# Mixture-of-experts tail: pairs with rows of the first 24 chunks first, two thirds of the sums read ahead of the last product

## The chip, the cores and the metric

The kernel runs on one core of one Trainium2 chip. The metric is the device time of one execution in microseconds (us). TensorE is PE in the profile, VectorE is DVE, ScalarE is ACT, GpSimd is POOL and SyncE is SP. SP and ACT also issue plain transfers, POOL the indirect ones.

## What is computed

Three layers follow each other on an image of 2 x 256 channels x 48 x 48 positions: a mix of local attention and convolution, a state-space layer, and a layer of eight experts of which each position uses two. The change is in the last one and in what follows it. In the terms of the reference (its body is given here in short):

```
xn      = layernorm(x)                                  # 4608 positions x 256
logits  = xn @ Wg + bg                                  # 8 experts
e1, e2  = the two best experts, weights by softmax over the two
y[pos]  = x[pos] + sum over e in (e1, e2) of
          weight_e * (gelu(xn[pos] @ W1[e] + b1[e]) @ W2[e] + b2[e])     # 256 -> 1024 -> 256
out     = y as 2 x 256 x 48 x 48
```

All values are float32.

## The kernel before, in words

**Rows and tables.** The 4608 positions are 36 chunks of 128. The state-space layer works through the chunks in order, in groups of 6, 6, 6, 6, 6, 4 and 2. Behind each group `gate` (line 1524) picks the two experts of each position and `put` (line 1676) scatters the normalized row into a table `xs` in HBM, in which each expert has its own part and the rows of an expert stand in the order of the chunks. `taken` counts the rows of each expert. The residual of each chunk goes to `acc` in HBM (`keep`, line 1507), to which the experts add.

**Early tiles.** After four groups, 24 chunks, `early_expert` (line 1691) picks the expert with the most rows so far, and three tiles of 256 rows of it are computed during the last groups (`early_tile`, line 1744: products at lines 1802 and 1818, addition at 1830, scaling at 1837, scatter into `acc` at 1840). `ahead` holds the rows that this takes from that expert, `begin` where the rest of each expert begins.

**Planning.** `plan` (line 1852) turns the counts into two small tables with a chain of DVE instructions on all partitions: for each of 33 pairs (256 rows of one expert) and up to 8 singles (128 rows), the row of the table and the place of the expert's weights. The pairs stand in the order of the experts. The tables lie in the SBUF of the input `x[1]`, and SP reads an entry into a register (`value`, line 1936) ahead of each load.

**The tiles of the experts.** `experts` (line 1950) runs 37 tiles: 33 pairs, with a single behind every eighth pair, so that the last tile is a pair; up to four more singles stand in a branch that is taken only if there are more than four. For tile i, `load` (line 1978) brings the expert's weights (2 MB, a ring of three buffers) and `fetch` (line 1990) its rows; both are issued on SP three tiles ahead. `turn` (line 1997) transposes the rows. `up` (line 2043) makes the first product (line 2051) and the Gelu on ACT (line 2055). `down` makes the second: a single in eight plain products (line 2076) and one addition of the bias (line 2077), a pair in seven products of half the size instead of eight (line 2089, in the manner of Strassen and Winograd), from sums of weights (`weight_sums`, line 2016) and of hidden values (`hidden_sums`, line 2031) that DVE makes, followed by eight additions (lines 2094 to 2102). `finish` (line 2057) scales each 128 x 256 result on ACT (line 2060) and scatters it on POOL with an addition in HBM (line 2061). Two scatters of one tile are not ordered to each other; scatters of different tiles are.

**The results.** `results` (line 2142) runs after the branch. It reads `acc` in twelve blocks of three chunks (line 2152, alternating between SP and ACT) into the SBUF of `x`, transposes them on PE (line 2163), copies each result from PSUM, one half on DVE and one on ACT (line 2166), and writes 128 x 768 values at a time to `out` (line 2169, alternating between SP and ACT).

**What sets the order.** In the layers before, a planner writes the order of PE, DVE, ACT and SP out by cost and due time. In the expert stage the framework orders the instructions of each engine by itself from the order of the program and its dependencies; each engine works through its list in order, and an instruction that waits for a semaphore holds what is behind it. SP reads registers and issues its transfers in program order where the code asks for it. `declare_no_dep` and `add_to_no_dep_group` take the wait between named groups of transfers away.

Of the kernel before, what the change touches and what calls it, by code (L numbers as in the profile page):

```python
# [37 lines left out]
P = 128  # L38
# [26 lines left out]
NJ = 3  # L65
# [13 lines left out]
NUSUAL = E // 2  # L79
NROWS = E * PART + TR  # L80
# [146 lines left out]
class Kernel:  # L227
# [1463 lines left out]
    def early_expert(self, seen):  # L1691
# [9 lines left out]
        def of(name):  # L1701
            return T["e", name]
# [4 lines left out]
                new("count", E), T["before", EARLY + 1][:, 0, :], self.c["base"], ALU.subtract)),  # L1707
            ("DVE", 205, lambda: vec.tensor_reduce(new("most", 1), of("count"), AX.X, ALU.max)),
            ("DVE", 205, lambda: tt(new("hot", E), of("count"), of("most").to_broadcast(wide), ALU.is_equal)),
# [3 lines left out]
            ("POOL", 200, lambda: pool.tensor_tensor(of("count"), of("hot"), self.c["tid"][:, :E], ALU.mult)),  # L1713
# [138 lines left out]
    def plan(self):  # L1852

        nc, begun = self.nc, [5 * TR] * NH
        n, k, tid = P, CAP // TR, self.c["tid"]
        tri = self.c["tri"].rearrange("p (a b) -> p a b", a=E)

        def new(*shape, dtype=F32):
            size = int(np.prod(shape))
            h = next(h for h in range(NH) if begun[h] + size <= N)  # L1860
            t = self.x[1][:, h, begun[h] : begun[h] + size]
            begun[h] += size
            if len(shape) > 1:
                names = "abc"[: len(shape)]
                t = t.rearrange(f"p ({' '.join(names)}) -> p {' '.join(names)}", **dict(zip(names[1:], shape[1:])))
            return t.bitcast(dtype) if dtype != F32 else t

        last_rows = new(E, dtype=I32)
        nc.vector.tensor_scalar(last_rows, self.taken, 1.0, None, ALU.add)
        rows = new(2, E)  # L1870
        nc.vector.tensor_sub(rows[:, 0, :], self.taken, self.begin)
        nc.vector.tensor_scalar(rows[:, 1, :], rows[:, 0, :], float(-P), None, ALU.add)
        full, ab = new(2 * E, k), new(2, E)
        shape = [n, 2 * E, k]
        flat = rows.rearrange("p i e -> p (i e)")
        nc.vector.tensor_tensor(full, bcast(flat, 2, shape), bcast(self.c["thr"], 1, shape), ALU.is_gt)
        nc.vector.tensor_reduce(ab.rearrange("p i e -> p (i e)"), full, AX.X, ALU.add)
        nc.vector.tensor_scalar(ab[:, :, 0:1], ab[:, :, 0:1], 1.0, None, ALU.max)

        def ends(name, count):  # L1880
            each, end = new(E, E), new(E)
            nc.vector.tensor_tensor(each, bcast(count, 1, [n, E, E]), tri, ALU.mult)
            nc.vector.tensor_reduce(end, each, AX.X, ALU.add)
            return end

        def places(name, end, count):

            shape = [n, count, E]
            done, which, begin = new(count, E), new(count), new(count)
            last = new(count, E)  # L1890
            nc.vector.tensor_tensor(done, bcast(tid[:, :count], 2, shape), bcast(end, 1, shape), ALU.is_ge)
            nc.vector.tensor_reduce(which, done, AX.X, ALU.add)
            nc.vector.tensor_tensor(last, done, bcast(end, 1, shape), ALU.mult)
            nc.vector.tensor_reduce(begin, last, AX.X, ALU.max)
            nc.vector.tensor_sub(begin, tid[:, :count], begin)
            return done, which, begin

        pend = ends("p", ab[:, 1, :])
        nc.vector.tensor_scalar(pend, pend, float(NPAIR), None, ALU.min)
        done, pwhich, prow = places("p", pend, NPAIR)  # L1900
        nc.vector.tensor_scalar(prow, prow, float(TR), None, ALU.mult)

        pairs, left = new(E + 1), new(E)
        nc.vector.memset(pairs[:, E:], 0.0)
        nc.vector.tensor_copy(pairs[:, 0:1], pend[:, 0:1])
        nc.vector.tensor_sub(pairs[:, 1:E], pend[:, 1:], pend[:, : E - 1])
        nc.vector.tensor_add(left, ab[:, 0, :], ab[:, 1, :])
        nc.vector.scalar_tensor_tensor(left, pairs[:, :E], -2.0, left, ALU.mult, ALU.add)
        send = ends("s", left)
        many = new(1, dtype=I32)  # L1910
        nc.vector.tensor_copy(many, send[:, E - 1 :])
        done, swhich, srow = places("s", send, NSINGLE)
        step, behind = new(E), new(NSINGLE)
        nc.vector.tensor_sub(step, pairs[:, 1:], pairs[:, :E])
        nc.vector.tensor_tensor(done, done, bcast(step, 1, [n, NSINGLE, E]), ALU.mult)
        nc.vector.tensor_reduce(behind, done, AX.X, ALU.add)
        nc.vector.tensor_scalar(behind, behind, pairs[:, 0:1], 2.0, ALU.add, ALU.mult)
        nc.vector.tensor_add(srow, srow, behind)
        nc.vector.tensor_scalar(srow, srow, float(P), None, ALU.mult)
        where = []  # L1920
        for name, which, row in (("p", pwhich, prow), ("s", swhich, srow)):
            to = new(2, which.shape[-1], dtype=I32)
            nc.vector.scalar_tensor_tensor(row, which, float(PART), row, ALU.mult, ALU.add)
            count = which.shape[-1]
            shape = [n, count, E]
            own, past = new(count, E), new(count)
            nc.vector.tensor_tensor(own, bcast(which, 2, shape), bcast(tid[:, :E], 1, shape), ALU.is_equal)
            nc.vector.tensor_tensor(own, own, bcast(self.ahead, 1, shape), ALU.mult)
            nc.vector.tensor_reduce(past, own, AX.X, ALU.add)
            nc.vector.tensor_add(row, row, past)  # L1930
            nc.vector.tensor_scalar(to[:, 0, :], row, float(E * PART), None, ALU.min)
            nc.vector.tensor_scalar(to[:, 1, :], which, float(E - 1), float(P), ALU.min, ALU.mult)
            where.append(to)
        return last_rows, where, many
# [15 lines left out]
    def experts(self, ctx):  # L1950
# [9 lines left out]
        every = NPAIR // NUSUAL  # L1960
        for i in range(NPAIR):
            tiles.append((2, i))
            if i % every == every - 1:
                tiles.append((1, i // every))
        usual = len(tiles)
        tiles += [(1, i) for i in range(NUSUAL, NSINGLE)]
# [49 lines left out]
        def weight_sums(i):  # L2016


            if i >= len(tiles) or tiles[i][0] == 1:
                return  # L2020
# [36 lines left out]
        def finish(i, y, j):  # L2057
# [7 lines left out]
            self.tc.add_to_no_dep_group(f"tile{i}", put.ins)  # L2065

        def down(i):
# [4 lines left out]
            if tiles[i][0] == 1:  # L2072
                y = hp.tile([P, C], F32, tag="ey", name="ey", bufs=5)
                po = banks[0][:, :C]
                for c in range(NHC):
                    nc.tensor.matmul(po, lhsT=hid[:, c, :P], rhs=w2[:, c, :], start=c == 0, stop=c == NHC - 1)  # L2076
                nc.vector.tensor_add(y, po, b2)
                finish(i, y, 0)
# [40 lines left out]
        def run(first, end):  # L2119
            for i in range(first, end):  # L2120
                up(i)
                if i + 1 < end:
                    turn(i + 1)
                if tiles[i][0] == 2:
                    hidden_sums(i)
                down(i)
                if i + 1 < end:
                    weight_sums(i + 1)
                if i + 3 < end:
                    fetch(i + 3)  # L2130
                    load(i + 3)

        run(0, usual)

        with self.tc.If(self.value(many[0:1, 0:1], list(self.nc.engines), NSINGLE) > NUSUAL):
# [4 lines left out]
            run(usual, len(tiles))  # L2140

    def results(self, ctx):

        nc = self.nc
        op = self.pool("o", 12, ctx)

        blocks = []
        for g in range(B * NBLK):
            b, blk = divmod(g, NBLK)
            t = self.x[b].rearrange("p k n -> p (k n)")[:, blk * NJ * C : (blk + 1) * NJ * C]  # L2150
            t = t.rearrange("p (j c) -> p j c", j=NJ)
            (nc.sync, nc.scalar)[g % 2].dma_start(
                t, self.acc[g * TB : (g + 1) * TB, :].rearrange("(p j) c -> p j c", j=NJ)
            )
            blocks.append(t)
        for g in range(0, B * NBLK, 2):
            b, blk = divmod(g, NBLK)
            for k in range(NH):
                o = op.tile([P, 2, TB], F32, tag="o", name="o")
                for i in range(2):  # L2160
                    ps = self.bank()
                    for j in range(NJ):
                        nc.tensor.transpose(
                            ps[:, j * P : (j + 1) * P], blocks[g + i][:, j, k * P : (k + 1) * P], self.ident
# [6 lines left out]
    def run(self):  # L2171
# [35 lines left out]
        self.ahead = up.tile([P, E], F32, name="ahead")  # L2207
        self.pick = up.tile([P, 4], I32, name="pick")
# [6 lines left out]
        with ExitStack() as end:  # L2215
            self.results(end)
# [87 lines left out]
```

## Time and profile before

| | us |
|---|---|
| median of three runs before | 1310.37 |
| these runs, lowest and highest | 1309.21, 1315.11 |
| the profiled execution, its own time | 1316.04 |
| span of the profiled execution | 1314.3 |
| PE busy | 1232.6 (94%) |
| DVE, ACT, POOL busy | 930.9, 797.9, 557.2 |
| first product of the expert stage begins (line 2051) | 799.77 |
| last product ends (line 2089) | 1277.35 |

The span is the time from the first to the last instruction; the profiled execution's own time is a little longer. The lines of the timeline give the start in us, the length in us, the engine, the line of the kernel, the operation, the destination and source by name, their shapes and how many equal instructions are merged; in brackets stands how long the engine was idle before, and what ended that. SPq and ACTq are the instructions that issue transfers; their length is that of the issuing and not of the transfer. A table of stretches gives, for a stretch, its length, the busy time and number of instructions of PE, PEld (weight loads), DVE, ACT and POOL, the granted clock of PE as a share of full speed, the busy share of the 16 DMA engines and the GB/s they moved.

### The profile page before, as it was taken

The numbers are of one execution on the slowest core, as the hardware profiler recorded it, in microseconds if no ns is written. First come the engines' busy times: TensorE is split into PE (matmuls) and PEld (weight loads), VectorE is DVE, ScalarE is ACT, GpSimd is POOL, SyncE is SP. The second block draws the span as 40 slices with busy tenths as digits, with TensorE's granted clock in tenths as the row PEclk, the third lists the DMA queues.
The fourth block names the chain that finished last, engine by engine and source line by source line (L and its number), as shares of the span: only waits on it lengthen the run. The fifth ranks groups of instructions, "written<-read, shape, count | busy, mean of one in ns | idle before, by whom it ended". The sixth has DMA issues, their size and how long they took to land.

```text
span 1314.3 us, 23601 instructions
## 1 busy us (share of the span) xinstructions
PE 1232.6 (94%) x8072; PEld 981.6 (75%) x8072; DVE 930.9 (71%) x2427; ACT 797.9 (61%) x1957; POOL 557.2 (42%) x769
## 2 busy tenths in 40 slices
PE   4999999996999999999999979999999999999983
PEld 3566767664667766677666758999999999999982
DVE  5899999998587878888878644565565556556642
ACT  2598978897899887987787633233334333332332
POOL 4312230211367798989888872122212121221220
PEclk9999999999899999999999999999999999999997
DMA  8331322210232242426346147567756766776628
GB/s 295 109 103 41 123 75 88 64 49 30 71 93 84 87 140 85 145 80 193 111 139 181 58 140 255 174 212 230 227 177 227 236 200 190 229 236 185 211 39 297
DMA packets 101659, 194.13 MB, mean 148 GB/s; under 512 B 10635, under 2 KB 82652, under 8 KB 96604
## 3 DMA queue, kind: packets, MB, share of 16 engines
q1 hardware_dynamic: 84156, 166.15, 37.7%
q0 software_dynamic: 14400, 19.74, 7.7%
q10 hardware_dynamic: 2980, 6.69, 1.3%
q8 instruction: 66, 1.08, 0.3%
q14 instruction: 57, 0.47, 0.1%
HBM read 154.24 MB, written 43.23 MB: 150 GB/s over the span
## 4 chain that ended last, share of the span: by engine, by line
PE 40%; POOL 10%; DMA 5%; issue 3%; ACT 3%; DVE 3%; SPq 0%; ACTq 0%; DVEq 0%; POOLq 0%
PE bank L2051 17%; PE po L2089 14%; DMA acc<-ey,token 4%; POOL xs L1676 3%; POOL sq L1455 1%; PE bank L914 1%; POOL y L1440 1%; PE bank L1818 1%; PE bank L900 1%; PE zbank L914 1%; POOL y L1422 1%; PE bank L1802 1%; PE bank L1448 1%; PE po L2076 1%; DMA out<-o 1%
## 5 line engine op out<-in xcount | busy, mean ns | idle before, releaser
L2061 POOL DMA_INDIRECT acc<-ey,token x70 | 109.1, 1559 | 370.3 <-ACT ey L2060 330.4
L2051 PE MATMUL bank<-ext,wt 128*128 128x256 f32 (+1 forms) x1152 | 241.3, 368 | 0.0
L2055 ACT ACTIVATE hid<-bank,bt 128x256 f32<-128x256 f32 (+1 forms) x288 | 132.9, 463 | 170.4 <-PE bank L2051 166.4
L2051 PEld LDWEIGHTS bank<-ext,wt 128*128 128x128 f32 x1152 | 207.0, 190 | 25.0
L679 POOL COPY kp<-kp 128x10 f32<-128x10 f32 (+1 forms) x60 | 24.7, 411 | 178.8 <-DVE kp L672 178.8
L590 DVE SCALAR_TENSOR_TENSOR x<-hid,w2r,x 128x1128 f32<-128x1128 f32 (+3 forms) x72 | 100.0, 1394 | 0.4 <-ACT hid L584 0.2
L2089 PE MATMUL po<-ts,ss 128*128 128x128 f32 x792 | 99.2, 275 | 0.0
L914 PE MATMUL bank<-xn,win 128*128 128x387 f32 x240 | 92.4, 508 | 2.1 <-ACT t L996 2.1
L2089 PEld LDWEIGHTS po<-ts,ss 128*128 128x128 f32 x792 | 93.7, 192 | 0.0
L1126 DVE SCALAR_TENSOR_TENSOR xc<-bank,vec,xc 128x384 f32<-128x384 f32 x144 | 86.7, 612 | 9.3 <-ACT xc L1115 8.7
L1342 ACT ACTIVATE mt<-mt,cum 128x128 f32<-128x128 f32 x288 | 88.2, 395 | 0.0
L798 ACT ACTIVATE prob<-prob,top 128x308 f32<-128x308 f32 x144 | 78.6, 554 | 15.7 <-DVE top L787 15.5
L2093 ACT COPY u<-po 128x128 f32<-128x128 f32 x33 | 8.8, 267 | 117.0 <-PE po L2089 117.0
L1676 POOL DMA_INDIRECT xs<-u,rows x72 | 72.6, 1009 | 16.1 <-issue 14.4
L2038 DVE TENSOR_TENSOR ss<-hid 128x512 f32<-128x512 f32 x33 | 22.8, 691 | 72.7 <-ACT hid L2055 72.7
L1448 PE MATMUL bank<-wout,y 128*128 128x264 f32 x288 | 70.8, 390 | 1.2 <-DVE yi L1407 1.2
L914 PE MATMUL zbank<-xn,win 128*128 128x384 f32 x192 | 71.0, 491 | 0.3 <-ACT z L1244 0.3
L804 ACT ACTIVATE prob<-prob,rden 128x308 f32<-128x308 f32 x144 | 68.0, 552 | 3.6 <-DVE rden L853 3.6
L580 DVE SCALAR_TENSOR_TENSOR hid<-xp,vec,hid 128x1175 f32<-128x1175 f32 (+1 forms) x48 | 68.5, 1427 | 0.1
L2089 PE MATMUL po<-wt,hid 128*128 128x128 f32 x512 | 67.6, 275 | 0.0
L787 DVE CUSTOM_DVE_ANT_0 prob<-banks,cst 128x308 f32<-128x308 f32 x144 | 61.7, 473 | 3.9 <-PE banks L777 3.6
L2089 PEld LDWEIGHTS po<-wt,hid 128*128 128x128 f32 x512 | 62.3, 192 | 0.1
(324 smaller groups left out, 2972.6 us busy)
## 6 DMA issues: line engine op xcount, KB each, us to landing
wt<-in_We SPq DMA_DIRECT2D x36, 2048.0 KB
mt<-decays SPq DMA_DIRECT2D x36, 512.0 KB
ex<-xs SPq DMA_DIRECT2D x36, 265.0 KB
rd<-decays SPq DMA_DIRECT2D x68, 128.0 KB
val<-vtab SPq DMA_DIRECT2D x72, 110.0 KB
bt<-in_We SPq DMA_DIRECT2D x36, 136.0 KB
vraster<-vout SPq DMA_DIRECT2D x18, 256.0 KB
acc<-x SPq DMA_DIRECT2D x36, 128.0 KB
```

The costliest lines, as they stand in the source:

```text
L580: nc.vector.scalar_tensor_tensor(dst, src, w[:, k : k + 1], dst, ALU.mult, ALU.add)
L590: nc.vector.scalar_tensor_tensor(dst, src, w[:, k : k + 1], dst, ALU.mult, ALU.add)
L798: nc.scalar.activation(t, t, AF.Exp, bias=T["top", c][:, a : a + 1], scale=-1.0, accum_out=T["den", c][:, a : a + 1])
L914: self.nc.tensor.matmul(ps, lhsT=lhs(k), rhs=rhs(k), start=k == 0, stop=k == NH - 1)
L1126: nc.vector.scalar_tensor_tensor(out(), T["bank", ("cv", at)][:, i : i + TB], wc[:, i : i + 1], out(), ALU.mult, ALU.add)
L1342: nc.scalar.activation(t, t, AF.Relu, bias=at_s, scale=-1.0)
L1448: nc.tensor.matmul(ps[:, : C + E], lhsT=T["y", c][:, m, :], rhs=self.l1["wout"][:, m, :], start=m == 0, stop=m == NZ - 1,)
L1676: ins = nc.gpsimd.indirect_dma_start(self.xs, bass.IndirectOffsetOnAxis(ap=of("rows")[:, i, q : q + 1], axis=0), T["u2", g][:, i, :], None,)
L2051: nc.tensor.matmul(ps[:, :rows], lhsT=w1[:, k, c * P : (c + 1) * P], rhs=xt[:, k, :], start=k == 0, stop=k == NH - 1,)
L2055: nc.scalar.activation(hid[:, c, :], ps[:, :rows], AF.Gelu, bias=bt[:, c : c + 1])
L2061: put = nc.gpsimd.indirect_dma_start(self.acc, bass.IndirectOffsetOnAxis(ap=token[:, j : j + 1], axis=0), y, None, compute_op=ALU.add)
L2089: nc.tensor.matmul(p[name], lhsT=v[a][:, c], rhs=v[w][:, c], start=c == 0, stop=c == NHC // 2 - 1)
```

## The change

- **Order of the pairs.** `plan` gets a second count for each expert: the pairs with a row of the first 24 chunks (`seen`, now kept, less `ahead`, in units of 256 rows, rounded up, and at most the pairs that the expert has). The table of pairs lists these of all experts first, at most 28 of them by the counts, and then the rest of all experts, so that it has up to 16 parts instead of 8. The number of pairs and singles stays.
- **Singles.** A single stands behind every seventh of the first 28 pairs, so the last five tiles are pairs whose rows are all of later chunks.
- **Reads of the first 24 chunks.** The eight blocks of the first 24 chunks are read from `acc` behind the loads of the last tile, all on SP. Their wait for the scatters of the last five tiles is taken away. Blocks 6 to 11 go to another part of `x[1]`. The branch for more singles reads the eight blocks once more at its end.
- **Last tile.** The last pair is computed with plain products in two halves, without the sums of weights and of hidden values.
- **Results.** They no longer have buffers of their own but use the ring of the weights, five of 128 x 768 in one. The last four blocks are read, in program order, behind the code of the first eight.

The core of the diff; the planning is cut to what counts the pairs:

```diff
+BEFORE = sum(GROUPS[: EARLY + 1])
+NFIRST = (BEFORE * 2 * P - NEARLY * TR) // TR + E - 1
...
+        rows = new(3, E)
...
+        vec.tensor_sub(rows[:, 2, :], self.seen, self.ahead)
+        full, ab = piece(3 * E, k), new(3, E)
...
+        first = ab[:, 2, :]
+        vec.tensor_tensor(first, first, ab[:, 1, :], ALU.min)
...
+        pend, second = new(2 * E), new(E)
+        vec.tensor_sub(second, ab[:, 1, :], first)
+        ends(pend[:, :E], first)
+        ends(pend[:, E:], second)
+        vec.tensor_tensor(pend[:, E:], pend[:, E:], pend[:, E - 1 : E].to_broadcast([n, E]), ALU.add)
+        vec.tensor_scalar(pend, pend, float(NPAIR), None, ALU.min)
+        done, pwhich, prow = places(pend, NPAIR)
+        late = new(NPAIR)
+        vec.tensor_scalar(late, pwhich, float(E), None, ALU.is_ge)
+        vec.scalar_tensor_tensor(pwhich, late, float(-E), pwhich, ALU.mult, ALU.add)
...
-        every = NPAIR // NUSUAL
+        every = NFIRST // NUSUAL
         for i in range(NPAIR):
             tiles.append((2, i))
-            if i % every == every - 1:
+            if i < NFIRST and i % every == every - 1:
                 tiles.append((1, i // every))
         usual = len(tiles)
+        last_pairs = usual - (NPAIR - NFIRST)
+        nfirst, load_sums = BEFORE // NJ, self.load_sums
...
-            if i >= len(tiles) or tiles[i][0] == 1:
+            if i >= len(tiles) or tiles[i][0] == 1 or i == usual - 1:
                 return
...
             self.tc.add_to_no_dep_group(f"tile{i}", put.ins)
+            if last_pairs <= i < usual:
+                self.tc.declare_no_dep(put.ins, group="first sums", reason="the last pairs have rows of later chunks")
...
-            if tiles[i][0] == 1:
-                y = hp.tile([P, C], F32, tag="ey", name="ey", bufs=5)
-                po = banks[0][:, :C]
-                for c in range(NHC):
-                    nc.tensor.matmul(po, lhsT=hid[:, c, :P], rhs=w2[:, c, :], start=c == 0, stop=c == NHC - 1)
-                nc.vector.tensor_add(y, po, b2)
-                finish(i, y, 0)
+            if i not in sums:
+                for j, bank in enumerate(banks):
+                    y = hp.tile([P, C], F32, tag="ey", name="ey", bufs=5)
+                    po = bank[:, :C]
+                    for c in range(NHC):
+                        nc.tensor.matmul(
+                            po, lhsT=hid[:, c, j * P : (j + 1) * P], rhs=w2[:, c, :], start=c == 0, stop=c == NHC - 1
+                        )
+                    nc.vector.tensor_add(y, po, b2)
+                    finish(i, y, j)
...
                 if i + 3 < end:
                     fetch(i + 3)
                     load(i + 3)
+                if i + 4 == usual:
+                    for g in range(nfirst):
+                        load_sums(g, "first sums")
...
             turn(usual)
             run(usual, len(tiles))
-
-    def results(self, ctx):
+            for g in range(nfirst):
+                load_sums(g)
+        self.results(ew)
+
+    def sums_block(self, g):
+
+        b, at = divmod(g, NBLK)
+        if b == 0:
+            t = self.flat(0)[:, at * NJ * C : (at + 1) * NJ * C]
+        else:
+            i, h = divmod(at, NH)
+            t = self.x[1][:, h, i * NJ * C : (i + 1) * NJ * C]
+        return t.rearrange("p (j c) -> p j c", j=NJ)
+
+    def load_sums(self, g, group=None):
...
+        get = (nc.sync, nc.scalar)[g % 2 if group is None else 0].dma_start(
+            self.sums_block(g), self.acc[g * TB : (g + 1) * TB, :].rearrange("(p j) c -> p j c", j=NJ)
+        )
+        if group:
+            self.tc.add_to_no_dep_group(group, get.ins)
+
+    def results(self, pool):
...
+        first, size, n = BEFORE // NJ, 2 * TB, 0
         for g in range(0, B * NBLK, 2):
             b, blk = divmod(g, NBLK)
+            if g == first:
+                for i in range(first, B * NBLK):
+                    self.load_sums(i)
             for k in range(NH):
-                o = op.tile([P, 2, TB], F32, tag="o", name="o")
+                if n % (WMAT // size) == 0:
+                    space = pool.tile([P, WMAT], F32, tag="wt", name="o")
+                o = space[:, n % (WMAT // size) * size :][:, :size].rearrange("p (i t) -> p i t", i=2)
+                n += 1
```

## The prediction

> **What bounds the kernel now.** I read the page first, for which engine fills which part of the span, then the timeline and busy time by stretch for the last 50 us, then the timeline around the start of the expert stage, where the enlarged planning runs.
>
> ```profile
> span 1314.3 us, 23601 instructions
> ...
> PE   4999999996999999999999979999999999999983
> ...
> DMA  8331322210232242426346147567756766776628
> ```
>
> Each digit is a fortieth of the span, 32.9 us. PE is full until the last slice but one; the last slice has PE at 3 and DMA at 8. So PE sets the pace until the last product, and something with the DMA engines sets it after that. The timeline shows the joint:
>
> ```profile
> 1276.29 1.06 PE L2089 MATMUL po<-wt,ss 128*128 128x128 f32 x8
> ...
> 1278.70 0.75 DVE L2102 TENSOR_TENSOR ey<-ey,bt 128x256 f32<-128x256 f32 x2
> ...
> 1281.80 1.55 POOL L2061 DMA_INDIRECT acc<-ey,token  x1 [0.31 <-issue]
> ...
> 1285.77 6.05 SPq L2152 DMA_DIRECT2D x<-acc  x6
> 1286.07 7.07 ACTq L2152 DMA_DIRECT2D x<-acc  x6
> ...
> 1294.64 0.34 ACTq L2169 DMA_DIRECT2D out<-o  x1
> ...
> 1306.46 0.34 ACTq L2169 DMA_DIRECT2D out<-o  x1
> ```
>
> The last product ends at 1276.29 + 1.06 = 1277.35 us. Then come the sums of the seven products on DVE, the scaling on ACT and two scatters on POOL, the second ending at 1281.80 + 1.55 = 1283.35. The first read of the sums (line 2152) starts 2.42 us later, once the scatter has landed. From 1285.77 to 1314.3, 28.53 us, twelve reads and twelve writes of 384 KB run. The whole tail behind the last product is 1314.3 - 1277.35 = 36.95 us. By stretch (columns: stretch, length, busy time of PE, PEld, DVE, ACT, POOL, PE clock, DMA share, GB/s):
>
> ```profile
> 1277.50:1285.60 8.10, 0.00 (x0) 0.00 (x0) 1.93 (x8) 0.91 (x2) 3.10 (x2) 0.71 0.29 32
> 1285.60:1288.00 2.40, 0.00 (x0) 0.00 (x0) 0.00 (x0) 0.00 (x0) 0.00 (x0) 0.50 0.48 126
> 1288.00:1311.00 23.00, 12.00 (x72) 9.47 (x72) 7.66 (x12) 7.16 (x12) 0.00 (x0) 0.80 1.02 394
> 1311.00:1314.30 3.30, 0.00 (x0) 0.00 (x0) 0.00 (x0) 0.00 (x0) 0.00 (x0) 0.50 0.09 37
> ...
> 1255.00:1257.00 2.00, 2.00 (x20) 2.00 (x19) 1.13 (x2) 0.00 (x0) 0.00 (x0) 1.00 0.00 0
> ```
>
> For 23 us the DMA share is 1.02: the tail is bound by bytes at 394 GB/s, with 2.40 us of start and 3.30 us of run-out. The last line is inside the last tiles: PE full, DMA 0, since no weights are left to load. The change puts reads there.
>
> **What the Trainium skill says.** "DMA: Bandwidth & Descriptors", section "Issuing engines are not separate DMA queues", says that transfers issued by SP, ACT and POOL end up on the same 16 DMA engines; the trace agrees, the 23 us being full with two issuers. Its section "Anatomy of one DMA — SWDGE (gpsimd) path" puts about 2.0 us of a transfer down to fixed cost, mostly confirmation of the write; the 2.42 us between scatter and read agrees. "Perfetto Trace Analysis", "Sequencer Loop", has a sequencer read its next instruction and wait for its semaphores, which is why I looked at what stands behind each new wait; the first ACT copy of the results idling 13.3 us behind DMA x<-acc fits that.
>
> **The change, part by part.** I call the end of the last product T (1277.35) before and T' after.
>
> *Eight reads moved.* They stand on SP behind the weights of the last pair, which before are issued at 1243.37, when the buffer of three tiles earlier comes free. Three pairs then follow, each with a pitch of 13.60 us (two starts of line 2051: 1202.38 and 1215.98). Nothing else stands behind them on SP before the branch. They bring 8 x 384 KB = 3.15 MB into a stretch with about 41 us. With the last pair's 2.3 MB this is 5.5 MB, 14 us at 394 GB/s, and the weights come first; their first use is about 27 us after issue. I cost the reads at nothing; the cover is this slack, and without it each us by which the last weights are late is a us. They must wait only for scatters of tiles before the last five, which landed long ago. The tail loses 3.15 MB / 394 GB/s = **8.0 us**. If the tail's dip at 1296 to 1300 (359 and 301 GB/s against 410 beside it) goes too, 0.7 us more; I take half, 0.35.
>
> *Last tile with the plain product.* Line 2076 on 128 rows took 3.62 us (1260.57 to 1264.19). Two such are 7.24, against 6.42 for the seven products (1270.93 to 1277.35): **+0.8 us** on PE, on the path. In exchange only one 0.42 us addition (line 2077), starting 0.03 after the product, 0.04 of handover, 0.51 of scaling, 0.27 of handover, 1.55 on POOL and 2.42 of landing follow: 5.24 us, since the first half was sent while PE did the second. Before this was 1285.77 - 1277.35 = 8.42. Gain **3.2 us**.
>
> *Order around the branch.* In the build the last four reads do not stand behind the early writes. On SP two of them come ahead of every write; on ACT one comes ahead of its first copy. All wait for the last scatter. Queued behind them are SP's six writes, ACT's twelve copies and its six writes; PE waits for those copies once its four banks are full. So two thirds are not written out at once: no write starts before T' + 5.24 plus about 1.3 us for a read to issue and a 0.6 us copy. I therefore give nothing for early writing. Can ACT then feed the DMA engines? Before, two copies and an issue repeated every 2.17 us (1296.78 and 1298.95), and SP issues one more in that time: 786 KB / 2.17 us = 362 GB/s, and the 1.57 MB of four reads fill the gap to 394 for longer than the remaining stretch. So bytes still bound it: 28.53 - 8.0 - 0.35 = 20.2 us.
>
> *Planning.* The build has 61 planning instructions on DVE instead of 48, with rows of 528 (about 0.71 us each, from 0.43 for 264 and 0.69 for 512) and 432.
>
> ```profile
> 781.11 0.17 DVE L1786 TENSOR_REDUCE eweight<-eown 128x2 f32<-128x16 f32 x1 [8.94 <-POOL eown L1778]
> ...
> 785.30 1.36 SPq L1995 DMA_DIRECT2D ex<-xs  x2
> ...
> 785.53 0.69 DVE L1830 TENSOR_TENSOR x<-bank,wt 128x512 f32<-128x512 f32 x1 [2.54 <-PE bank L1818]
> ...
> 787.72 0.34 SPq L1987 DMA_DIRECT2D wt<-in_We  x1
> ...
> 798.42 0.69 DVE L1830 TENSOR_TENSOR x<-bank,wt 128x512 f32<-128x512 f32 x1 [12.20 <-PE bank L1818]
> ```
>
> DVE stood idle 8.94 us ahead of line 1786, behind POOL's scatters; what is ahead of it in the new order, about 1 us more, is hidden. Behind it now stand 31 planning instructions, before 13 (1.9 us). At 0.13 to 0.21 us each, 0.35 to 0.4 for five of 264, this is 5.8 us: done near 787.0. The addition of line 1830 moves from 785.53 to 787.0, its scaling ends before ACT's next work at 789.85, and the weights of line 1987 go out 1.5 us later; they are first read at 812.78. PE waits for neither: cost nothing, at most the 3.9 us by which all this grows if a bank is missed.
>
> *Order of pairs, kept counts, buffers.* 33 pairs and four singles remain, each loading its weights as before; singles move from places 9, 18, 27, 36 to 8, 16, 24, 32. In the trace PE's only wait from 800 to 1278 is 0.9 us at the first tile: nothing. The results now use weight buffers: the first is free, the second free at the last product: nothing.
>
> **Sum.** 36.95 becomes 0.8 + 5.24 + 20.2 = 26.2, that is -10.7 us, less 0.2 for a first write that starts 1.3 us after the reads: **-10.5**. The profiled execution took 1316.04 us, 1.74 around its span, so it would be 1305.5. The median shown is 1310.37, 0.4% lower, with other executions from 1309.21 to 1315.11; I take the same difference: 1299.9.
>
> **Rivals.**
> 1. *Writes do start behind the last product*, as the change says. For: PE and DVE may begin right away. Against: the order above. Writes from T' + 3, first byte 1.5 us on, 6.3 MB at 410 GB/s = 15.3, run-out 3.3: T' + 23.1, gain 13.0: 1297.4.
> 2. *The eight reads still wait for the last scatters*, if the waits count more than the tiles before the last five. Then 28.53 stays and 3.2 - 0.8 = 2.4 are left: 1308.0. Against: the exclusion is declared on both sides. For: the waits of the read name all eight scatter semaphores, and up to which scatter they count does not show in the order.
> 3. *Planning costs in full*, 3.9 us (with 1.5 us more on the first weights, 5): 1304.
> 4. *Slower: the last pair's weights come late.* The place is the stretch from their issue to their use, 27 us for 5.5 MB. PE waits as soon as both share less than 204 GB/s; the gain is gone at 5.5 MB / 37.5 us = 147 GB/s. At 120 GB/s it is 46 us, 19 late, 8 slower than before: 1319. For: the mean over the span is only 148 GB/s. Against: that is demand; the same weights moved at 319 to 426 GB/s between 1245 and 1249, and they are first in the queue.
>
> **How the numbers follow.** Forecast 0.70, rivals 0.08, 0.12, 0.05, 0.05. The forecast's own range, 1296.5 to 1303, comes from 0.7 us for the dip, 1 to 2 us in the landing of the scatter, and 2.5 us between medians. 0.5% is 6.6 us, about what a measurement of this kernel can tell from no change, so faster means below 1303.8. Faster: 0.69 + 0.08 + 0.03 of the third = 0.80. Same: 0.01 + 0.12 + 0.02 = 0.15. Slower 0.05. The range reaches from rival 1 to rival 3: 1295.5 to 1305.
>
> **What would show it.** After: eight reads of acc some 40 us before the last product, with DMA no longer at 0 there; four reads behind the last scatter, ahead of any write; the stretch of full DMA near 15 us; last product to the reads 5.2 us instead of 8.4; the first product of the expert stage still near 799.8 us. Eight reads behind the last scatter would show rival 2, writes ahead of it rival 1, PE idle between the tiles rival 4. I would be wrong if the tail is not bound by bytes any more but by ACT's twelve copies and its issues, which at 1.08 us each need 13 us of the 20.

## The result, and the profile after

| | before | after |
|---|---|---|
| median, us | 1310.73 (9 runs, 1308.23 to 1315.11) | 1306.41 (9 runs, 1303.03 to 1308.44) |
| ratio of the times | | 0.9959, 95% interval 0.9942 to 0.9977 |
| the profiled execution, us | 1316.04 | 1306.41 |
| first product of the expert stage | 799.77 | 800.23 |
| last product ends | 1277.35 | 1278.46 |
| last product to end of span | 36.9 | 25.9 |

The ratio means 5.4 us less, between 3.0 and 7.6 (the two medians of the table alone differ by 4.3). The forecast of 1299.9 and its range up to 1305.0 were too low. The two profiled executions, however, differ by 9.6 us, close to the 10.5 of the sum. That contradiction is what the experiments had to settle: either the medians or the pair of profiles mislead.

The page of the changed kernel, the lines that answer to those of before:

```profile
span 1304.4 us, 23542 instructions
...
PE   4999999997899999999999998999999999999995
...
DMA  8331322211132243424446148567667657766756
```

PE's last slice now holds 5 tenths instead of 3. The end of the timeline of the changed kernel:

```profile
1271.39 7.07 PE L2108 MATMUL po<-wt,hid 128*128 128x256 f32 x32
...
1278.50 0.42 DVE L2111 TENSOR_TENSOR ey<-po,bt 128x256 f32<-128x256 f32 x1 [3.03 <-PE po L2108]
...
1279.97 1.55 POOL L2090 DMA_INDIRECT acc<-ey,token  x1 [2.13 <-ACT ey L2089]
...
1283.92 1.22 SPq L2195 DMA_DIRECT2D x<-acc  x2
...
1284.42 0.67 ACT L2222 COPY o<-bank 128x384 f32<-128x384 f32 x1 [4.90 <-DMA acc<-ey,token]
...
1285.27 11.68 SPq L2225 DMA_DIRECT2D out<-o  x6
```

The last product ends at 1278.46, the first late read goes out 5.46 us later (8.42 before), and the first write only behind it, 6.8 us behind the last product. ScalarE's first copy idles 4.90 us because a read stands ahead of it in its list. The stretches of the changed kernel (columns as in the prediction):

```profile
1278.50:1283.90 5.40, 1.88 (x15) 1.60 (x15) 2.42 (x4) 0.51 (x1) 1.55 (x1) 1.00 0.41 51
...
1286.30:1301.20 14.90, 8.11 (x49) 6.00 (x47) 5.54 (x9) 5.69 (x10) 0.00 (x0) 0.84 1.01 385
1301.20:1304.40 3.20, 0.00 (x0) 0.00 (x0) 0.00 (x0) 0.00 (x0) 0.00 (x0) 0.50 0.25 101
1255.00:1257.00 2.00, 2.00 (x11) 1.77 (x10) 0.84 (x2) 1.26 (x3) 1.70 (x2) 1.00 1.05 420
```

The stretch of full DMA engines shrank from 23 to 14.9 us, and the reads lie where DMA stood at 0 before (last line). SP's own list, and its longest waits in the same 30 us:

```profile
1247.65 4.09 SPq L2195 DMA_DIRECT2D x<-acc  x8
```

```profile
SPq L2195 <- DMA acc<-ey,token: 9.6, 1, 9.6
```

The eight reads went out 31 us ahead of the end of the last product, not 40. They waited 9.6 us for a scatter: SP moves on 0.28 us after the second scatter of the fourth tile from the end has landed (POOL issued the two at 1241.22 and 1243.08, the second landed at 1247.37). So, by the times, the exclusion did not reach all of the last five tiles. It cost nothing here: PE has no gap from the first to the last product of the stage.

### The profile page after: what moved, and what is told of

It reads as the page before. It is cut to its first block, busy times and chain, and to the rows that moved or that the text cites. A ratio compares the mean times of both kernels' runs of the same rounds, so it can differ in the third digit from the quotient of the medians.

```text
span 1304.4 us, 23542 instructions
## 1 busy us (share of the span) xinstructions
PE 1237.6 (95%) x8048; PEld 984.3 (75%) x8048; DVE 929.0 (71%) x2425; ACT 796.3 (61%) x1956; POOL 557.9 (43%) x769
## 4 chain that ended last, share of the span: by engine, by line
PE 46%; POOL 10%; DVE 3%; issue 3%; ACT 2%; DMA 1%; ACTq 0%; SPq 0%; DVEq 0%; POOLq 0%
PE bank L2080 19%; PE po L2123 15%; POOL xs L1678 4%; PE bank L916 2%; PE bank L1450 1%; PE po L2108 1%; PE bank L902 1%; PE zbank L916 1%; POOL sq L1457 1%; POOL y L1424 1%; POOL y L1442 1%; PE bank L1820 1%; PE bank L1432 1%; PE bank L1804 1%; POOL y L1331 1%
## 5 line engine op out<-in xcount | busy, mean ns | idle before, releaser
L2123 PE MATMUL po<-ts,ss 128*128 128x128 f32 x768 | 96.2, 275 | 0.0
L2123 PEld LDWEIGHTS po<-ts,ss 128*128 128x128 f32 x768 | 90.9, 192 | 0.0
L916 PEld LDWEIGHTS bank<-xn,win 128*128 128x128 f32 x240 | 43.2, 196 | 23.9 <-issue 3.7
```

Of the source, the lines that this page charges most:

```text
L916: self.nc.tensor.matmul(ps, lhsT=lhs(k), rhs=rhs(k), start=k == 0, stop=k == NH - 1)
L2123: nc.tensor.matmul(p[name], lhsT=v[a][:, c], rhs=v[w][:, c], start=c == 0, stop=c == NHC // 2 - 1)
```

## The experiments

The front is here the time up to the first product of the expert stage, the tail the time behind the last one. Theory A: the front pays part of the gain back in most executions, and the one profile of before hid that. B: the tail of that profile was long by chance. C: the medians differ by the draw of runs.

**Both kernels once more** (no edit).

> The kernel before, unchanged, for the time, the last product and the tail of another execution of it. Both profiles shown so far give the change 9.9 us (span 1314.3 to 1304.4), the medians give it about 5. Theory A (the front pays back: the tail is shorter by 11 us in every run, and the way to the last product is longer by about 4 to 5 us in most, which the one profile of before hid because its own way was slow): ratio 1.000, last product ending near 1272 to 1274 us, tail 36 to 37 us. Theory B (the tail of the profiled run was long by chance): ratio 1.000, last product near 1277, tail near 32 us. Theory C (the medians differ only by the draw of runs): last product near 1277 and tail near 37.

> The changed kernel, unchanged, timed in one call with the kernel before. Theory A: ratio 0.9955 to 0.9965 (5 us faster), last product ending 4 to 5 us later than in the repeat of before, tail 26 us. Theory B: ratio the same, last product 1 us later than in the repeat of before, tail 26 us. Theory C: ratio near 0.992 (10 us faster), last product 1 us later, tail 26 us.

Measured: before 1.0006 of itself (0.9995 to 1.0017), changed 0.9952 (0.9938 to 0.9967), that is 6.3 us less. Last product at 1276.45 and 1275.58, tail 36.4 and 26.1 us. The tails repeat, so B falls; the ratio repeats, so C falls. But the last product of the changed kernel ends 0.9 us earlier than that of before, not 4 to 5 us later, as Theory A had said. Whole executions differ by too much to show that: up to the end of DVE's wait for POOL (line 1786, in the changed kernel 1788, see below) the thirteen profiles of this case need between 780.31 and 784.84 us, and the three with the old planning (781.11, 782.18, 784.52) lie among the others. No loss ahead of that wait shows. A front has to be compared inside a short stretch, from this wait on. Just ahead of the expert stage, the repeat of before shows this (DVE, then ACT, then PE):

```profile
784.52 0.17 DVE L1786 TENSOR_REDUCE eweight<-eown 128x2 f32<-128x16 f32 x1 [8.93 <-POOL eown L1778]
...
786.30 0.68 DVE L1830 TENSOR_TENSOR x<-bank,wt 128x512 f32<-128x512 f32 x1
```

```profile
775.79 0.59 ACT L1790 COPY x<-bank 128x512 f32<-128x512 f32 x1 [2.72 <-PE bank L1802]
...
787.02 0.91 ACT L1837 ACTIVATE x<-x,eweight 128x256 f32<-128x256 f32 x2 [6.88 <-DVE x L1830]
787.84 1.55 ACT L1810 ACTIVATE x<-bank,wt 128x256 f32<-128x256 f32 x4
```

```profile
788.34 2.67 PE L1818 MATMUL bank<-wt,x 128*128 128x256 f32 x8 [2.23 <-ACT x L1810]
790.80 2.95 PE L1802 MATMUL bank<-x,wt 128*128 128x256 f32 x8
```

The addition follows the wait for POOL by 1.8 us, ACT scales its result, and the Gelus behind that in ACT's list (line 1810) release PE. PE already idles 2.23 us for them. The same place in the changed kernel, in the same order:

```profile
782.18 0.17 DVE L1788 TENSOR_REDUCE eweight<-eown 128x2 f32<-128x16 f32 x1 [8.93 <-POOL eown L1780]
...
786.75 0.68 DVE L1832 TENSOR_TENSOR x<-bank,wt 128x512 f32<-128x512 f32 x1
```

```profile
787.47 0.91 ACT L1839 ACTIVATE x<-x,eweight 128x256 f32<-128x256 f32 x2 [9.83 <-DVE x L1832]
788.29 1.55 ACT L1812 ACTIVATE x<-bank,wt 128x256 f32<-128x256 f32 x4
```

```profile
788.79 3.78 PE L1820 MATMUL bank<-wt,x 128*128 128x256 f32 x8 [5.18 <-ACT x L1812]
792.37 3.03 PE L1804 MATMUL bank<-x,wt 128*128 128x256 f32 x8
```

Now 4.6 us lie between, and PE idles 5.18 us. And the profile of before that the prediction was made from (ACT, then PE):

```profile
778.24 0.59 ACT L1790 COPY x<-bank 128x512 f32<-128x512 f32 x1 [8.51 <-remote]
...
786.26 0.91 ACT L1837 ACTIVATE x<-x,eweight 128x256 f32<-128x256 f32 x2
789.85 0.84 ACT L1810 ACTIVATE x<-bank,wt 128x256 f32<-128x256 f32 x2 [2.68 <-PE bank L1802]
```

```profile
778.88 3.54 PE L1802 MATMUL bank<-x,wt 128*128 128x256 f32 x8 [4.81 <-issue]
```

Here ACT stood for 8.51 us on something that the profile only calls remote, and PE 4.81 us. No other of the thirteen profiles has this. In the repeat ACT's copy starts 0.04 us behind the product of line 1802 that it waits for, here 5.9 us behind the same product; and PE goes on 0.05 us after the copy has ended. So PE's wait looks like a consequence of ACT's. It delayed the products that the addition waits for, so that the addition came 4.4 us behind the wait for POOL, as late as the longer planning makes it. The stall was the cover.

**New planning and order of pairs alone.** The changed kernel with the reads, results and last tile of before:

```diff
-                if i + 4 == usual:
-                    for g in range(nfirst):
-                        load_sums(g, "first sums")
...
-            if i >= len(tiles) or tiles[i][0] == 1 or i == usual - 1:
+            if i >= len(tiles) or tiles[i][0] == 1:
...
+        with ExitStack() as end:
+            self.results(end)
```

> The new planning and order of pairs alone, with the reads, the results and the last tile of the kernel before. The forecast gave this part nothing. Theory A: 4 to 5 us slower than before (ratio 1.003 to 1.004), lost ahead of the last product. Theories B and C: within 1 us of before (ratio 0.9995 to 1.001).

Measured: 1.0038 (1.0023 to 1.0052), 5.0 us slower than before, as Theory A said. PE idles 5.14 us ahead of line 1820, and from the first to the last product of the stage it takes 477.6 us, as before (477.6 and 477.9): the order of the pairs costs nothing there.

**All reads late.**

```diff
-                if i + 4 == usual:
-                    for g in range(nfirst):
-                        load_sums(g, "first sums")
...
-            for g in range(nfirst):
-                load_sums(g)
+        for g in range(nfirst):
+            load_sums(g)
```

> The changed kernel with all twelve reads behind the last tiles; planning, order of pairs and plain last tile stay. By the byte count of the forecast the eight early reads are worth 8.0 us: the tail behind the last product is 34 us instead of 26. Theories A and C: 8 us slower than the changed kernel. Theory B: about 4 us slower, as the tail would then not be bound by bytes alone.

Measured: 1.0016 (1.0006 to 1.0026), tail 33.1 us. Against the changed kernel that is 7.0 to 7.2 us of tail, and 7.5 to 8.4 us by the two ratios. The bytes count as forecast.

**Planning behind the addition.** Two theories of the place: A1, the planning holds up the second early tile's addition and through it PE; A2, the front loses its time ahead of that. The last part of `plan`, from `send` on, is issued behind the addition, in the changed kernel and in the kernel before:

```diff
+            if i == 1:
+                self.second_add = self.last_add
...
-        send = ends(new(E), left)
+        with self.tc.issue_after(self.second_add.ins):
+            send = ends(new(E), left)
```

> The changed kernel with the last part of the planning issued behind the second early tile's addition (line 1832 of the changed kernel), so that only the tail end of it delays the tables and not the addition. Theory A1 (the new planning holds up that addition, the addition holds up the scaling on ScalarE, the scaling holds up the activations that free PE's banks, and PE idles 5.18 us there instead of 2.23): PE's idle time ahead of the product at about 787 falls to under 1.5 us, the halved clock behind it is shorter, and the kernel is 3 to 5 us faster than the changed kernel: ratio to before 0.992 to 0.993. Theory A2 (the front loses its time to the later place and taken rows ahead of the planning): no change, 0.9955. Against both: weights of the second tile go out some 3 us later, and if that is seen PE idles ahead of 812.

> The kernel before with the last part of its own planning behind the second early tile's addition. Theory A1: its 13 instructions behind the wait for POOL cost the same way, only less: PE idle there falls from 2.23 us to under 1.5 us, and the kernel is 1 to 2.5 us faster than before (ratio 0.998 to 0.999). Theory A2: no change (1.000).

Measured: changed kernel 0.9904 (0.9884 to 0.9924), 12.6 us below before; kernel before 0.9990 (0.9982 to 0.9998), 1.3 us below itself. PE of the changed kernel with later planning:

```profile
785.84 1.99 PE L1820 MATMUL bank<-wt,x 128*128 128x256 f32 x8 [0.66 <-ACT x L1812]
787.67 1.89 PE L1804 MATMUL bank<-x,wt 128*128 128x256 f32 x8
```

The wait is gone, and the same sixteen products take 3.9 us instead of 6.8. A1 holds, A2 falls. The gain, 6.3 to 7.2 us against the changed kernel, is larger than the 3 to 5 us expected: from the wait for POOL to the first product it is 7.4 us less than in the changed kernel's first profile, 4.5 us of that idle time and 2.9 us slower products, which the expectation had counted too low. Part of it is given back: PE waits 0.6 us (1.2 us in the kernel before) in the first tiles of the stage. The tables come later in these two kernels; that this is the reason is not shown.

**Planning longer.** One sum is made seven times more, with the same result:

```diff
-            vec.tensor_reduce(past, hot, AX.X, ALU.add)
+            for _ in range(1 if behind is None else 8):
+                vec.tensor_reduce(past, hot, AX.X, ALU.add)
```

> The changed kernel with one sum of the planning (line 1956 of the changed kernel, 128x33 from 128x264, 0.42 us, a start every 0.34 us) made seven times more with the same result, between the wait for POOL and the second early tile's addition: 2.4 us more on VectorE, less what then slips behind the addition. Theory A1: PE's idle time at about 787 grows from 5.2 us by 2.1 to 2.4 us, and the time by the same, up to 1.7 us more if the clock stays halved longer: ratio to before 0.9970 to 0.9990 (the changed kernel 0.9952 to 0.9959). Theory A2 or any other place in front: no change.

```profile
792.51 3.78 PE L1820 MATMUL bank<-wt,x 128*128 128x256 f32 x8 [7.83 <-ACT x L1812]
```

Measured: 0.9975 (0.9964 to 0.9985), 2.1 to 3.0 us above the changed kernel; the intervals overlap, so the trace has to carry this. PE's idle time grew by 2.65 us, as much as the addition was moved (2.7 us). The dose shows: what DVE puts between the wait for POOL and the addition comes back one for one as idle time of PE. Side by side (us; the last column is from the start of the `eweight` sum behind POOL to the first product of the stage):

| kernel | DVE instructions between | to the addition | PE idle | next 8 + 8 products | to first product |
|---|---|---|---|---|---|
| before, the profile shown | 13 | 4.4 | 4.81 and 1.75 | | 18.7 |
| before, repeat | 13 | 1.8 | 2.23 | 2.67 + 2.95 | 14.1 |
| changed | 31 | 4.6 | 5.18 | 3.78 + 3.03 | 18.1 |
| changed, repeat | 31 | 4.6 | 5.18 | 3.57 + 1.89 | 16.7 |
| new planning alone | 31 | 4.6 | 5.14 | 3.78 + 2.65 | 17.7 |
| planning longer | 36 | 7.3 | 7.83 | 3.78 + 1.97 | 19.7 |
| planning later, changed | 0 | 0.1 | 0.66 | 1.99 + 1.89 | 10.7 |
| planning later, before | 0 | 0.1 | 0.36 | 1.99 + 1.89 | 10.7 |

**Seven products in the last pair.**

```diff
-            if i >= len(tiles) or tiles[i][0] == 1 or i == usual - 1:
+            if i >= len(tiles) or tiles[i][0] == 1:
```

> The changed kernel with the seven products kept for the last pair. By the forecast the plain product costs 0.8 us on PE and saves 3.2 us behind it: this kernel is 2.4 us slower than the changed kernel (ratio to before about 0.997), with 8.4 us from the last product to the first late read instead of 5.5. If the second half of the seven products hides behind nothing that matters: within 0.5 us of the changed kernel.

Measured: 0.9972 (0.9960 to 0.9984), 1.7 to 2.6 us above the changed kernel, with overlapping intervals. The trace is clearer: from the last product to the first late read 8.43 us, to the end 28.8 (25.9 in the changed kernel); the expert stage is 0.65 us shorter on PE. As forecast.

**Last reads on POOL.**

```diff
-        get = (nc.sync, nc.scalar)[g % 2 if group is None else 0].dma_start(
+        get = (nc.gpsimd if pool else nc.sync if group else (nc.sync, nc.scalar)[g % 2]).dma_start(
...
-                    self.load_sums(i)
+                    self.load_sums(i, pool=True)
```

> The changed kernel with the last four reads of the sums issued by POOL, so that they no longer stand ahead of the writes on SP and of the copies on ScalarE. If the order was what kept the writes back: first write 3 us behind the last product instead of 6.8, the last 6.3 MB end 23.1 us behind the last product instead of 25.9: 2.5 to 3 us faster than the changed kernel (ratio to before about 0.993). Rival: POOL [...]issues them one after the other, so that the last block comes later and takes the gain back: within 1 us of the changed kernel.

```profile
1281.70 17.32 SPq L2225 DMA_DIRECT2D out<-o  x6
...
1284.35 2.29 POOL L2195 DMA_DIRECT2D x<-acc  x4 [2.88 <-DMA acc<-ey,token]
...
1290.97 2.79 PE L2219 MATMUL bank<-cst,x 128*128 128x128 f32 x12 [5.67 <-DMA x<-acc]
```

The stretch that follows (columns as in the prediction):

```profile
1291.00:1300.00 9.00, 6.84 (x30) 5.86 (x30) 2.69 (x4) 3.89 (x6) 0.00 (x0) 0.50 0.79 312
```

The changed kernel, for comparison, at its first late block:

```profile
1291.93 2.58 PE L2219 MATMUL bank<-cst,x 128*128 128x128 f32 x18 [1.09 <-DMA x<-acc]
```

Measured: 0.9954 (0.9938 to 0.9970), no change. The tail is 25.1 us, 0.9 to 1.1 us less. The writes do start 3.3 us behind the last product. But the first late block is used 6.6 us after POOL begins to issue the reads (8.0 us after the first late read in the changed kernel), with the DMA share at 1.01 from 1284 to 1291. By then PE has nothing left to transpose and waits 5.67 us. Behind that wait its granted clock is 0.50, twelve transposes take 2.79 us (eighteen took 2.58 us in the changed kernel), and in the 9 us from 1291 on the DMA share is only 0.79. The outcome that the rival named holds, but not its reason: POOL issues four reads in 2.29 us. The late block comes while reads and writes share full DMA engines; how much of the lost time is due to that and how much to the lowered clock, these runs do not separate.

**Four writes first**, on top of the later planning, with that kernel once more beside it:

```diff
-            if g == first:
-                for i in range(first, B * NBLK):
-                    self.load_sums(i)
+            if g == 4:
+                with self.tc.issue_after(puts[-2].ins), self.tc.issue_after(puts[-1].ins):
+                    for i in range(first, B * NBLK):
+                        self.load_sums(i)
```

> The kernel with the later planning, and the last four reads of the sums put behind the first four writes (two on SP, two on ScalarE) instead of ahead of all. If the dead time from the last product to the first byte of the tail can be filled: writes start 3.3 us behind the last product as with the reads on POOL, 1.6 MB of them are through when the reads go out at 5.5 us, and the tail ends some 24 us behind the last product instead of 26: 2 us faster than the kernel with the later planning (ratio to before 0.989). Rival: the reads then share the DMA engines with the writes, the last blocks come later, and PE and the copies wait for them as with the reads on POOL: within 1 us (0.990).

> The kernel with the later planning once more, in one call with the kernel with four writes first, and for a second profile: ratio to before 0.9895 to 0.9915, PE idle under 1 us ahead of the product at about 786, no halved clock there, last product to end of the span 26 us.

Measured: 0.9909 (0.9894 to 0.9924) and 0.9911 (0.9896 to 0.9926). The tail of the one profile is 24.5 us against 26.3, but 0.8 us of that is lost in the first tiles of the stage, and the times do not differ. PE again waits 4.58 us for a block. Of the 1.7 us in the tail, 0.9 us are left over the stretch from the wait for POOL to the end; whether they are real stays open: the intervals are 2 us wide to each side. The later planning itself repeats; it is the version to keep, 12 us below the kernel before.

## Why the prediction was wrong

**Planning: the step that failed.** "PE waits for neither: cost nothing, at most the 3.9 us by which all this grows if a bank is missed." PE does wait, through ACT: the addition comes later, ACT's scaling with it, and the Gelus that release PE stand behind the scaling. New planning alone costs 5.0 us (3.0 to 6.8). The short stretch from the wait for POOL to the first product is 4.0 us longer in the changed kernel than in the repeat of before, some 2.95 of it PE's idle time and 1.2 the slower products behind it; over the six profiles with the whole new planning ahead of the addition it is 2.7 to 4.1 us longer, always against that one profile of before without the stall. The work itself was not put too low: 31 instructions take 4.6 us, and 5.8 were forecast. Rival 3 had the price (3.9) and the time (1304), at a chance of 0.05. Two readings went wrong. I asked what ACT does next at 789.85, in an execution in which ACT and PE had just been held up: there the Gelus behind the scaling had to wait 2.68 us for PE. In the others they are ready, and PE waits for them. And I took the gap ahead of the addition (2.54 us behind line 1818) for slack of the program, without asking why line 1818 came so late. The lines that answered that, ACT's 8.51 us behind "remote" and PE's 4.81 us behind "issue", were in the trace and not in my sum.

**From the profile to the median.** "The median shown is 1310.37, 0.4% lower [...] I take the same difference." The profiled execution carried 4.6 us (18.7 against 14.1) at the very place where the change puts its work. In that one execution the new planning would have been free; in the median it is not. So the pair of profiles agrees with the sum (1305.5 forecast, 1306.41 measured) and the medians do not; the agreement is luck. A pair of profiles proves little in any case: those of the two repeats are 11.2 us apart without any such stall, because the way up to the wait for POOL was 3.9 us longer in that execution of before. With the planning at 4.0 the sum is 6.5 us, against 5.4 (3.0 to 7.6) measured.

**Eight reads moved.** 8.35 us forecast, 7.0 to 7.2 in the tail. Right in the main. They go out 9 us later than said and wait for a tile that I took as excluded ("which landed long ago"); it is the harmless form of rival 2. Rival 4 did not show: PE has no gap.

**Last tile.** +0.8 and -3.2 forecast; +0.65 on PE, and 3.0 less to the first read, measured against seven products. Right.

**Order around the branch.** Reads ahead of the writes, first write behind them, 20.2 us from reads to end forecast, 20.5 measured. Right; and rival 1, 13.0 us for writes that start at once, falls: the first write of the changed kernel went out 6.8 us behind the last product, and where the writes do start at 3.3 us, the tail is 25.1 us and not 23.1.

**Order of pairs, buffers.** Nothing forecast, nothing found between the first and the last product.

With the planning moved out of the way in both kernels, the change is worth 1309.37 - 1299.21 = 10.2 us by the medians (11.3 by the two ratios), against 10.5 forecast. So the rest of the sum was right in its total.

**Open.** What held ACT in the profile of before. That it was there by chance is what twelve profiles without it suggest, two of them of kernels with the old planning.

## What to carry to other kernels

Before a step is costed at nothing, ask what makes its cover, and whether that cover belongs to the program: a wait that the profile puts down to "remote" or "issue" may be of that execution alone. A profiled time above all timed runs is a hint of it, but no more: the repeat of before took 1314.75 us without a stall. Work that an engine does between a late arrival and the next operand of another engine is on the path, however idle the engine was before; put it behind that operand. Bytes moved out of a tail that fills the DMA engines are gained nearly in full (7.0 to 7.2 us here, where the byte count said 8.0). Starting the writes early, while the last reads were still to come, shortened the tail by only 0.9 and 1.7 us here, and no measured time.

## What was not expected of the hardware

PE's idle time cost more than itself. The granted clock of PE in the same 20 us of three kernels, the changed one, the repeat of before, and the changed one with later planning:

```profile
780.00:800.00 20.00, 14.10 (x53) 11.39 (x51) 6.37 (x35) 3.59 (x9) 8.19 (x8) 0.83 0.78 225
```

```profile
780.00:800.00 20.00, 16.82 (x72) 13.97 (x71) 5.09 (x23) 4.44 (x12) 10.69 (x11) 0.91 0.74 226
```

```profile
780.00:800.00 20.00, 18.40 (x86) 15.66 (x86) 10.33 (x47) 6.61 (x16) 12.63 (x11) 1.00 0.76 205
```

At half speed while it is lowered, a mean of 0.83 is 20 x 0.17 / 0.5 = 6.8 us, 0.91 is 3.6 us and 1.00 none, behind idle times of 5.18, 2.23 and 0.66 us. Eight products of line 1820 then take 3.78 instead of 1.99 us. The length of the idle time alone does not decide: the repeat of the changed kernel, with the same 5.18 us, has a mean of 0.91. The repeat of before, more closely:

```profile
786.10:789.50 3.40, 1.17 (x6) 1.05 (x6) 0.85 (x3) 2.36 (x6) 2.79 (x3) 1.00 0.71 133
789.50:792.90 3.40, 3.40 (x9) 2.69 (x9) 0.00 (x0) 0.00 (x0) 2.08 (x2) 0.50 1.02 303
792.90:796.30 3.40, 3.40 (x17) 2.98 (x16) 0.00 (x0) 0.84 (x2) 0.00 (x0) 0.99 1.00 353
```

The clock falls 1.2 us after PE has gone on, and rises one step later. The Trainium skill says in "TensorE: Matmul & The Clock Gate", section "Part 1: The HAM clock gate (the "warmup" mystery)", that the clock is halved after about one idle window of 3.4 us, in windows that run freely. The trace agrees with the steps of about 3.4 us, and that the same idle time brought one step in one execution and two in another fits windows that run freely. But the 3.4 us ahead of this fall were not idle throughout: they held 1.17 us of products and 2.23 us of idle time, and that was enough for one step, less than the page says.
